# Layer 0's softmax with one exponential and sums on VectorE, and layer 1's head columns written by VectorE through a mask

## Chip, core and metric

The kernel runs on one core of a Trainium2 chip. The metric is the device time of one execution in microseconds (us). Five engines work side by side, each through its own queue of instructions in a fixed order: TensorE (PE, matrix products; its weight loads are listed as PEld), VectorE (DVE), ScalarE (ACT), GpSimd (POOL) and SyncE (SP, which here only issues transfers). An instruction waits, at the head of its queue, until the semaphores that it names have been raised by others.

## The reference, cut to what matters

Input x has 128 graphs of 64 nodes with 256 features, and all graphs share one adjacency matrix of 64x64. Four graph layers follow one another, each as `x = layernorm(x + layer(x))`. The change concerns the first two.

```python
# layer 0: attention over neighbours
Wh = h @ W
s1, s2 = Wh @ a1, Wh @ a2
e = s1[:, :, None] + s2[:, None, :]
e = where(e >= 0, e, 0.2 * e)
e = where(adj == 0, -inf, e)
h_prime = softmax(e, axis=-1) @ Wh

# layer 1: attention along 512 edges (src, dst), 4 heads of 64 features
Xq, Xv = H @ W_lin.T, H @ W_val.T                 # split into heads
e = einsum(leaky_relu(Xq[src] + Xq[dst], 0.2), a) + log(A0[src, dst] + 1e-8)
attn = softmax of e over the edges with the same src
Y = segment_sum(attn * Xv[dst], src) @ W_out.T
```

Layer 2 is a graph convolution with two batch norms, layer 3 two graph convolutions and four LSTMs with windows of 1 to 4 nodes; they take the last three quarters of the time and aren't touched.

## The kernel before

**Tiling.** Layers 0 and 1 run in one software pipeline over 16 blocks q. A block has 8 graphs: 512 tokens, as four chunks c of 128 tokens, so that a chunk holds two graphs (s = 0 in partitions 0 to 63, s = 1 in 64 to 127). Attention of layer 0 is computed for a chunk as one 128x128 matrix; `mask` is zero on the two 64x64 diagonal blocks where there is an edge, and -1e30 elsewhere.

**Layer 0 of a block** is in parts. `l0_a` (L238) turns x by a DVE transpose (L243). `l0_b` (L247) multiplies by W and copies the result out of PSUM by ACT (L255, L258). `l0_c` (L260) makes the scores e of [128, 4, 128] on DVE: sum with the mask (L267), leaky relu (L269), and the negated row maximum mx (L271). `l0_x` (L274) takes the exponential on ACT: one instruction for each of the four chunks, with mx as bias for each partition, and with the row sums collected by the same instruction (L278); the profile lists a READ_ACCUMULATOR after each. DVE then takes the reciprocal (L281). `l0_d` (L283) transposes the result on PE (L287) and copies it (L289, ACT). `l0_e` (L291) multiplies by Wh, scales and adds on DVE (L300) and normalises; `layernorm` (L88) does its statistics on DVE (L95, L96), a power on POOL (L86) and the scaling on POOL (L100).

**Layer 1 of a block.** `l1_t` (L310) transposes the tokens and copies them by ACT (L228). `l1_qv` (L314) makes queries and values of two chunks; it's called twice for a block. The product with wq (L324) has 260 columns: 256 queries and 4 head columns, a linear share of the score for each head. The queries go to `qs`, in two versions that hold one graph's rows as they are (a copy by ACT, L334) and for the other graph the remainder after rounding (a subtraction by DVE, L335). The head columns, times 0.2, go to `spad` (L336): one ACT instruction for each of the two graphs of a chunk, which writes the 4 columns of that graph's 64 rows; the other rows stay at the zero that they got at the start. The values (L327) are copied by ACT as `v` (L337). `l1_graph` (L356) gathers a graph's queries along the edges by a product with a one-hot matrix (L361, into one of two PSUM buffers z of two banks each) and applies relu on ACT (L363); `reduce_heads` sums over features (L352), and `l1_softmax`, `l1_sums`, `l1_weights` (L368 to L413) handle the softmax of two blocks together: a product with spad (L371), scans on DVE (L378 to L387), transposes (L395), reciprocal and weights on DVE (L401, L403), then a scatter into a table by POOL (L407) and a load back (L413). `v_a` (L422) multiplies values by weights (L432, copied by ACT as yT, L436), `v_b` (L438) multiplies by W_out (L446), adds (L448) and normalises, `v_c` (L454) multiplies by layer 2's adjacency (L467) and copies by ACT (L471).

**Order.** The loop over q (L701) has 8 steps, one for each graph of the block, and the table `between` (L703) says which parts of which other blocks come after each. S is the number of the pair of blocks whose layer 1 softmax is made in this step; it's there in even q from 2 on. In odd q, and in q=0, l0_x follows l0_c in the fifth group; in the other even q it stands in the sixth, after l1_qv, and `behind` (L692) orders it after the last ACT instruction recorded so far. `step` orders only PE: each part's first product comes after the part before it. A scheduler places the rest, engine by engine, as it estimates.

**Buffers.** Most products go into PSUM tiles called m, of one bank each, three in rotation (`bank`, L144): a product waits until every reader of the tile three before it is done.

Of the kernel before, what the change touches and what calls it, by code (L numbers as in the profile page):

```python
# [8 lines left out]
F32 = mybir.dt.float32  # L9
F32R = mybir.dt.float32r  # L10
I32 = mybir.dt.int32
AF = mybir.ActivationFunctionType
OP = mybir.AluOpType
AX = mybir.AxisListType
# [3 lines left out]
P = 128  # L18
NB = 128
N = 64  # L20
D = 256
KD = D // P
HEADS = 4
# [4 lines left out]
PQ = 4  # L28
QT = 512
GQ = 8  # L30
BPS = 2
# [6 lines left out]
SLOPE = 0.2  # L38
# [3 lines left out]
def kernel(ctx: ExitStack, tc: tile.TileContext, i, out):  # L42
    nc = tc.nc

    const = ctx.enter_context(tc.tile_pool(name="const", bufs=1))
    small = ctx.enter_context(tc.tile_pool(name="small", bufs=4))
# [83 lines left out]
    with ExitStack() as two:  # L130
# [5 lines left out]
        wa = two.enter_context(tc.tile_pool(name="wa", bufs=1))  # L136
# [7 lines left out]
        def bank(shape, name="m", bufs=3):  # L144
            return (psm if name == "m" else ps).tile([P] + shape, F32, name=name, bufs=bufs)
# [64 lines left out]
        count = wa.tile([P, EC], F32, name="count")  # L210
        place = wa.tile([P, EC], I32, name="place")
        spads = [wa.tile([P, P], F32, name=f"spad{n}") for n in range(2)]


        table = [dram.tile([PAIRS + E, SROWS], F32, name=f"table{n}") for n in range(2)]

        def own(q, shape, name):

            return work.tile(shape, F32, name=name, bufs=1) if q else su.tile(shape, F32, name)
# [16 lines left out]
        L0 = {}  # L236
# [37 lines left out]
        def l0_x(q):  # L274
            e, mx = L0[q]["e"], L0[q]["mx"]
            sm = small.tile([P, PQ], F32, name="sm")
            for c in range(PQ):
                nc.scalar.activation(e[:, c, :], e[:, c, :], AF.Exp, bias=mx[:, c:c + 1],  # L278
                                     accum_out=sm[:, c:c + 1])
            ri = L0[q]["ri"] = small.tile([P, PQ], F32, name="ri")  # L280
            nc.vector.reciprocal(ri, sm)  # L281

        def l0_d(q):  # L283
            e = L0[q]["e"]
            p_ = bank([PQ, P])
            for c in range(PQ):
                nc.tensor.transpose(p_[:, c, :], e[:, c, :], ident)  # L287
            eT = L0[q]["eT"] = own(q, [P, PQ, P], "eT")
            nc.scalar.activation(eT, p_, AF.Copy)  # L289
# [24 lines left out]
        def l1_qv(q, c2):  # L314
            xT, v = L1[q]["xT"], L1[q]["v"]

            sp = spads[q // BPS % 2].rearrange("p (s e x b d h) -> p s e x b d h", e=2, s=2, x=2, b=BPS, d=2)
            pv = None
            for c in (2 * c2, 2 * c2 + 1):
                pq = bank([D + HEADS])  # L320
                if pv is None:
                    pv = bank([2, D])
                for k in range(KD):
                    nc.tensor.matmul(pq, xT[:, k, c * P:(c + 1) * P], wq[:, k, :],  # L324
                                     start=k == 0, stop=k == KD - 1)
                for k in range(KD):
                    nc.tensor.matmul(pv[:, c % 2, :], xT[:, k, c * P:(c + 1) * P], wv[:, k, :],  # L327
                                     start=k == 0, stop=k == KD - 1)

                qs = work.tile([P, 2, D], F32R, name="qs", bufs=6)  # L330
                L1[q]["qs"].append(qs)
                for s in range(2):
                    r, ro = slice(s * N, (s + 1) * N), slice((1 - s) * N, (2 - s) * N)
                    nc.scalar.activation(qs[r, s, :], pq[r, :D], AF.Copy)  # L334
                    nc.vector.tensor_sub(qs[ro, s, :], pq[r, :D], qs[r, s, :].bitcast(F32))  # L335
                    nc.scalar.activation(sp[r, s, c % 2, 0, q % BPS, c // 2, :], pq[r, D:], AF.Copy, scale=SLOPE)  # L336
            nc.scalar.activation(v[:, 2 * c2:2 * c2 + 2, :], pv, AF.Copy)  # L337

        pes, pend = {}, []
# [26 lines left out]
        ld, sm = {}, {}  # L366
# [202 lines left out]
        setup_order()  # L569
        l0_c(0)  # L570
        l0_x(0)
        l0_a(1)
        setup_ends()
        l0_b(1)
        l0_d(0)
        setup_gather()
        setup_queries()
        l0_e(0)
        l0_c(1)
        l0_x(1)  # L580
        setup_signs()
        l0_d(1)
        l1_t(0)
        l1_qv(0, 0)
        l1_qv(0, 1)


# [91 lines left out]
        def step(do, n, *more):  # L679
            if not 0 <= n < NQ:  # L680
                return
            traced = nc.cur_bb.bb.instructions
            first = len(traced)
            if queue:
                with tc.issue_after(queue[-1]):
                    do(n, *more)
            else:
                do(n, *more)
            mine = [t for t in traced[first:] if t.engine == mybir.EngineType.PE]
            queue.extend(mine[-1:])  # L690

        def behind(do, q):  # L692
            if q < NQ:
                with tc.issue_after([t for t in nc.cur_bb.bb.instructions
                                     if t.engine == mybir.EngineType.Activation][-1]):
                    do(q)
# [4 lines left out]
        for q in range(NQ):  # L701
            S = q // BPS - 1 if q % BPS == 0 else -1
            between = [  # L703
                [(l0_e, q + 1), (l0_a, q + 2)],
                [(sums, q if q else -1), (l1_softmax, S)],
                [(l1_sums, S), (l0_b, q + 2)],
                [(v_b, q - LAG - 1)],
                [(l1_t, q + 1), (l1_weights, S), (l0_c, q + 2)] + [(l0_x, q + 2)] * (S < 0),
                [(sums, q), (l1_qv, q + 1, 0)] + [(lambda n: behind(l0_x, n), q + 2)] * (S >= 0),
                [(v_c, q - LAG - 1), (v_a, q - LAG)],  # L710
                [(l0_d, q + 2), (l1_qv, q + 1, 1)],
            ]
            for b in range(GQ):
                step(l1_graph, q, b)
                for do, n, *more in between[b]:
                    step(do, n, *more)
                if setup:
                    setup.pop(0)()
        sums(q)
        S = NQ // BPS - 1  # L720
# [256 lines left out]
        q = NQ - LAST - 1  # L977
# [16 lines left out]
        bias = wd.tile([P, SKIP, 8], F32, name="bias")  # L994
# [1010 lines left out]
```

## Time and profile before

| | |
|---|---|
| median of 3 runs | 2036.22 us (2034.6 to 2041.47) |
| the profiled execution's own time | 2039.12 us |
| its span, first to last instruction | 2037.3 us |
| mean granted clock of PE | 0.985 |

| stretch of the profiled execution (us) | what runs | PE busy | DVE busy | ACT busy | granted PE clock |
|---|---|---|---|---|---|
| 0 to 25 | loads, setup | 12.74 | 17.92 | 6.31 | 0.97 |
| 25 to 141 | setup, q = 0 to 2 | 98.67 | 68.45 | 70.94 | 0.92 |
| 141 to 475 | q = 3 to 13 | 318.73 | 197.08 | 225.10 | 0.99 |
| 475 to 525 | the last two q | 43.26 | 21.19 | 24.77 | 0.93 |
| 525 to 776 | layer 2 and the start of layer 3 | 240.97 | 144.18 | 112.65 | 0.97 |
| 776 to 2037.3 | layer 3 | 1225.69 | 799.18 | 548.23 | 1.00 |

The instructions that the change touches, over the whole execution or in the stretch from 125 to 475 us where that is said:

| line | engine, operation | shape | count | mean ns |
|---|---|---|---|---|
| L278, 125 to 475 | ACT exponential | 128x128 | 48 | 392 |
| L278, 125 to 475 | ACT read of the accumulator | 128x1 | 48 | 189 |
| L336, 125 to 475 | ACT head columns | 64x4 | 96 | 166 |
| L281, 125 to 475 | DVE reciprocal | 128x4 | 12 | 178 |
| L334, 125 to 475 | ACT copy of queries | 64x256 | 96 | 379 |
| L335 | DVE subtraction | 64x256 | 128 | 422 |
| L363 | ACT relu | 128x1024 | 128 | 1026 |

How to read it: the busy time of an engine in a stretch is the union of its instructions. In a line of the timeline come the start in us, the length in us, engine, line, operation, what it writes and reads, how many it merges, and in brackets the idle time of the engine before it with what ended it. In a list of waits come who waited for whom, the total in us, how often, and the longest. A row of the windows gives the stretch and its length, then for PE, PEld, DVE, ACT and POOL the busy time with the number of instructions, then PE's granted clock, the busy share of the transfer engines and GB/s.

### The profile page before, as it was taken

Reading aid. Unit: us, or ns where it says so; the run is one execution under the profiler, and the core shown is the slowest. Engines: PE = TensorE matmul, PEld = TensorE weight load, DVE = VectorE, ACT = ScalarE, POOL = GpSimd, SP = SyncE. Lnnn points to the kernel's source line nnn. Section 1 sums busy time; section 2 is a strip of 40 time slices with the busy share of each in tenths; the row PEclk is TensorE's granted clock in tenths of the full one; section 3 lists DMA queues with packets and bytes.
Section 4 is the critical chain, followed back from the end, with each engine's and each line's share of the span. In section 5 each row is a group of like instructions: output and inputs, shape, how many; then the busy total and the mean of one; then the engine's idle time right before and its main releaser. Section 6 shows DMA issues by size and latency. Waiting matters only on the chain.

```text
span 2037.3 us, 31496 instructions
## 1 busy us (share of the span) xinstructions
PE 1940.1 (95%) x11447; PEld 1337.8 (66%) x11447; DVE 1248.0 (61%) x2763; ACT 988.0 (48%) x1892; POOL 880.0 (43%) x1017
## 2 busy tenths in 40 slices
PE   5999999999999999899999999999999999999996
PEld 4667777766554445477678577667577668578685
DVE  7456565565456555765557865557775557664566
ACT  2766666666345633644343644333544333543333
POOL 1123333333445544564645543435543445444264
PEclk8999999999999998999999999999999999999999
DMA  5344443332302025433243243133143032132022
GB/s 129 85 67 65 83 68 55 66 45 39 51 22 60 38 93 185 148 139 107 86 162 92 66 155 136 39 132 88 58 152 121 24 111 66 47 119 78 0 62 73
DMA packets 236539, 173.84 MB, mean 85 GB/s; under 512 B 150624, under 2 KB 213600, under 8 KB 233056
## 3 DMA queue, kind: packets, MB, share of 16 engines
q1 hardware_dynamic: 234528, 169.86, 29.5%
q8 instruction: 90, 1.47, 0.3%
q0 software_dynamic: 1024, 1.05, 0.2%
q10 hardware_dynamic: 832, 0.92, 0.1%
q14 instruction: 65, 0.53, 0.1%
HBM read 110.18 MB, written 61.60 MB: 84 GB/s over the span
## 4 chain that ended last, share of the span: by engine, by line
PE 73%; DVE 14%; ACT 5%; DMA 3%; issue 3%; POOL 2%; SPq 1%; DVEq 0%; POOLq 0%; ACTq 0%
PE l L1728 27%; PE l L1684 8%; PE pz L845 4%; PE l L1463 4%; PE m L253 3%; PE pz L774 3%; PE m L324 3%; PE e L352 2%; PE m L446 2%; PE g L1362 2%; PE m L327 2%; PE z L361 2%; PE g L1350 2%; PE pz L1043 2%; DVE cell L1642 1%
## 5 line engine op out<-in xcount | busy, mean ns | idle before, releaser
L1728 PE MATMUL l<-hs,wh 128*128 128x256 f32 (+1 forms) x896 | 276.0, 399 | 3.7 <-DVE hs L1592 3.1
L1728 PE MATMUL l<-xs,wx 128*128 128x256 f32 (+1 forms) x896 | 276.2, 399 | 2.9 <-DVE gate L1747 2.7
L1743 ACT ACTIVATE kept<-l 128x256 f32<-128x256 f32 (+1 forms) x224 | 88.8, 403 | 333.2 <-PE l L1728 331.8
L86 POOL TENSOR_TENSOR ln_rs<-ln_rs,mhalf 128x2 f32<-128x2 f32 (+2 forms) x98 | 85.5, 873 | 367.4 <-DVE ln_rs L98 366.9
L1728 PE MATMUL l<-H,wx 128*128 128x256 f32 (+1 forms) x672 | 210.5, 402 | 4.3 <-DVE gate L1756 3.4
L1728 PE MATMUL l<-hid,wh 128*128 128x256 f32 (+1 forms) x672 | 208.7, 399 | 0.0
L1728 PEld LDWEIGHTS l<-hs,wh 128*128 128x128 f32 x896 | 169.1, 190 | 47.1 <-DVE hs L1592 5.7
L1728 PEld LDWEIGHTS l<-xs,wx 128*128 128x128 f32 x896 | 168.9, 190 | 46.1 <-issue 2.8
L1761 ACT ACTIVATE gate<-gate,bias 128x512 f32<-128x512 f32 (+1 forms) x280 | 170.6, 657 | 40.7 <-DVE gate L1752 34.8
L1684 PE MATMUL l<-H,wx 128*128 128x256 f32 (+5 forms) x672 | 185.2, 431 | 4.9 <-DVE H L116 2.7
L363 ACT ACTIVATE u<-z 128x1024 f32<-128x1024 f32 x128 | 130.3, 1026 | 68.8 <-PE z L361 67.7
L1684 PEld LDWEIGHTS l<-H,wx 128*128 128x128 f32 x672 | 118.8, 190 | 65.5 <-issue 34.2
L1728 PEld LDWEIGHTS l<-H,wx 128*128 128x128 f32 x672 | 125.7, 190 | 42.6 <-DVE gate L1756 7.4
L1728 PEld LDWEIGHTS l<-hid,wh 128*128 128x128 f32 x672 | 127.2, 190 | 32.0 <-issue 2.9
L1751 POOL TENSOR_TENSOR gate<-gate,kept 128x256 f32<-128x256 f32 (+1 forms) x84 | 65.1, 775 | 144.9 <-DVE kept L1749 136.2
L335 DVE TENSOR_TENSOR qs<-m,qs 64x256 fp32r<-64x256 f32 x128 | 54.0, 422 | 106.3 <-ACT qs L334 104.4
L361 PE MATMUL z<-gath_r,qs 128*128 128x512 f32 x256 | 100.4, 480 | 9.3 <-ACT u L363 8.9
L1756 DVE TENSOR_TENSOR gate<-l,gate 128x256 f32<-128x256 f32 (+1 forms) x112 | 50.0, 446 | 88.4 <-POOL gate L1751 64.3
L1596 POOL TENSOR_TENSOR hs<-hid 128x256 f32<-128x256 f32 (+1 forms) x28 | 26.0, 929 | 170.1 <-DVE hid L1628 87.0
L1650 ACT ACTIVATE gate<-cell 128x512 f32<-128x512 f32 (+1 forms) x88 | 58.6, 666 | 83.6 <-DVE cell L1642 61.5
L1638 POOL TENSOR_TENSOR cell<-gate,cell 128x512 f32<-128x512 f32 (+1 forms) x56 | 75.4, 1367 | 28.4 <-ACT gate L1761 28.4
L1745 DVE TENSOR_TENSOR gate<-l,kept 128x256 f32<-128x256 f32 (+1 forms) x112 | 49.1, 438 | 59.7 <-ACT gate L1761 32.6
(380 smaller groups left out, 4097.6 us busy)
## 6 DMA issues: line engine op xcount, KB each, us to landing
wx<-sums SPq DMA_DIRECT2D x9, 2048.0 KB
wh<-sums SPq DMA_DIRECT2D x9, 1792.0 KB
way<-st SPq DMA_DIRECT2D x54, 256.0 KB
st<-way SPq DMA_DIRECT2D x216, 64.0 KB
xin<-in_x SPq DMA_DIRECT2D x16, 512.0 KB
ld<-table SPq DMA_DIRECT2D x16, 512.0 KB
x_dram<-y SPq DMA_DIRECT2D x16, 512.0 KB
x2r<-x_dram SPq DMA_DIRECT2D x32, 256.0 KB
```

The source lines that it names most:

```text
L86: nc.gpsimd.tensor_tensor(dst, dst, mhalf[:, :n], OP.pow)
L253: nc.tensor.matmul(p_, xT[:, k, c * P:(c + 1) * P], w0[:, k, :], start=k == 0, stop=k == KD - 1)
L361: nc.tensor.matmul(z[:, k, :], L1[q]["qs"][c][:, s, k * P:(k + 1) * P], gath_r, start=True, stop=True)
L363: nc.scalar.activation(u, z, AF.Relu)
L845: nc.tensor.matmul(self.bank[at], lhs, rhs, start=first and n == 0, stop=n == len(self.terms) - 1, skip_group_check=True)
L1463: nc.tensor.matmul(self.bank[at], lhs, rhs, start=new, stop=True, skip_group_check=True)
L1638: nc.gpsimd.tensor_tensor(c, t, c, OP.mult)
L1684: nc.tensor.matmul(b, w.raw[0][:, k, at, m, :], x, start=k == 0, stop=k == KD - 1)
L1728: nc.tensor.matmul(self.banks[j], lhs, rhs, start=src == 0, stop=src == 1)
L1743: nc.scalar.activation(self.keep(j), b, AF.Copy)
L1751: e.tensor_tensor(t[0][:, 1], t[0][:, 1], k[5], OP.add)
L1761: given(lambda: nc.scalar.activation(dst, dst, f, bias=b))
```

## The change

Two edits, and one that follows from the first.

1. *Softmax of layer 0, blocks 2 to 15.* DVE adds the negated maximum to the whole e (512 elements a partition), ACT takes one exponential of the whole, and DVE sums the rows by a reduction. The sum and the reciprocal move from l0_x to l0_d, and the sum is ordered after the last DVE instruction recorded so far. Blocks 0 and 1 keep four exponentials with sums, but their reciprocal moves to l0_d too.
2. *Head columns.* A tile `slopes` of [128, 2, 4] holds 0.2 where the row belongs to graph s and 0 elsewhere; POOL writes it at the start. For each chunk one DVE product of the 4 columns (read twice from PSUM) with slopes writes the columns of both graphs, zeros included. The two ACT instructions are gone.
3. *Order.* l0_x now stands in the sixth group, after l1_qv and behind the last ACT instruction, in every q.

```diff
+        slopes = wa.tile([P, 2, HEADS], F32, name="slopes")
+        nc.gpsimd.memset(slopes, 0.0)
+        for s in range(2):
+            nc.gpsimd.memset(slopes[s * N:(s + 1) * N, s, :], SLOPE)
...
         def l0_x(q):
             e, mx = L0[q]["e"], L0[q]["mx"]
             sm = small.tile([P, PQ], F32, name="sm")
-            for c in range(PQ):
-                nc.scalar.activation(e[:, c, :], e[:, c, :], AF.Exp, bias=mx[:, c:c + 1],
-                                     accum_out=sm[:, c:c + 1])
+            if q < 2:
+                for c in range(PQ):
+                    nc.scalar.activation(e[:, c, :], e[:, c, :], AF.Exp, bias=mx[:, c:c + 1],
+                                         accum_out=sm[:, c:c + 1])
+            else:
+                nc.vector.tensor_add(e, e, mx[:, :, None].to_broadcast([P, PQ, P]))
+                nc.scalar.activation(e, e, AF.Exp)
+            L0[q]["sm"] = sm
+
+        def l0_d(q):
+            e, sm = L0[q]["e"], L0[q]["sm"]
             ri = L0[q]["ri"] = small.tile([P, PQ], F32, name="ri")
-            nc.vector.reciprocal(ri, sm)
-
-        def l0_d(q):
-            e = L0[q]["e"]
+            if q < 2:
+                nc.vector.reciprocal(ri, sm)
+            else:
+                with tc.issue_after([t for t in nc.cur_bb.bb.instructions if t.engine == mybir.EngineType.DVE][-1]):
+                    nc.vector.reduce_sum(sm, e, axis=AX.X)
+                nc.vector.reciprocal(ri, sm)
...
                     nc.scalar.activation(qs[r, s, :], pq[r, :D], AF.Copy)
                     nc.vector.tensor_sub(qs[ro, s, :], pq[r, :D], qs[r, s, :].bitcast(F32))
-                    nc.scalar.activation(sp[r, s, c % 2, 0, q % BPS, c // 2, :], pq[r, D:], AF.Copy, scale=SLOPE)
+                nc.vector.tensor_mul(sp[:, :, c % 2, 0, q % BPS, c // 2, :],
+                                     pq[:, None, D:].to_broadcast([P, 2, HEADS]), slopes)
...
-                [(l1_t, q + 1), (l1_weights, S), (l0_c, q + 2)] + [(l0_x, q + 2)] * (S < 0),
-                [(sums, q), (l1_qv, q + 1, 0)] + [(lambda n: behind(l0_x, n), q + 2)] * (S >= 0),
+                [(l1_t, q + 1), (l1_weights, S), (l0_c, q + 2)],
+                [(sums, q), (l1_qv, q + 1, 0)] + [(lambda n: behind(l0_x, n), q + 2)],
```

## The prediction, written before the changed kernel ran

> **What bounds the kernel now.** I read the page first (its shares of the span), then the windows by stage, then TensorE's waits in the stage that the change touches, and last the timeline of one even and one odd step of the loop over q.
>
> ```profile
> PE 1940.1 (95%) x11447; PEld 1337.8 (66%) x11447; DVE 1248.0 (61%) x2763; ACT 988.0 (48%) x1892; POOL 880.0 (43%) x1017
> ```
> ```profile
> 141.00:475.00 334.00, 318.73 (x2895) 234.97 (x2895) 197.08 (x517) 225.10 (x501) 121.18 (x137) 0.99 0.38 65
> ```
> ```profile
> PE z L361 <- ACT u L363: 8.6, 5, 1.8
> PE m L324 <- ACT yT L436: 4.0, 10, 0.6
> PE m L395 <- ACT tT L228: 1.5, 5, 0.3
> PE m L432 <- ACT v L337: 0.9, 1, 0.9
> ```
>
> TensorE (PE) sets the time: 95% of the span, and 318.7 of 334 us in the steady steps q=3 to q=13. So only PE's idle time there (15.3 us) and time lost to its clock can be won; ScalarE (ACT) and VectorE (DVE) each have a third of this stretch free. But all four waits of PE end on ACT. The largest comes five times, about 1.75 us each: PE waits for the relu L363, which frees one of the two z banks. In an even step (q=6):
>
> ```profile
> 246.33 0.81 PE L361 MATMUL z<-gath_r,qs 128*128 128x512 f32 x2
> 247.91 0.40 ACT L278 ACTIVATE e<-e,mx 128x128 f32<-128x128 f32 x1
> 249.89 1.02 ACT L363 ACTIVATE u<-z 128x1024 f32<-128x1024 f32 x1
> 250.81 1.02 ACT L471 ACTIVATE A<-z 128x1024 f32<-128x1024 f32 x1
> 250.96 0.75 PE L361 MATMUL z<-gath_r,qs 128*128 128x512 f32 x2 [1.79 <-ACT u L363]
> 251.71 1.09 ACT L436 ACTIVATE yT<-m 128x512 f32<-128x512 f32 x2
> 252.37 2.10 PE L324 MATMUL m<-wq,tT 128*128 128x260 f32 x4 [0.22 <-ACT yT L436]
> ```
>
> z was finished at 247.14, yet its relu began at 249.89: four exponentials and a head-column copy stood ahead of it in ACT's queue. Then the L324 group took 2.10 us; in the same place at 314.61 it takes 1.14. The windows row for 252.3 to 255.7 has PEclk at 0.50: the clock was halved after the stall. This happened in two of the five even steps (q=6 and q=10). In an odd step (q=7) the exponentials come early, the relu is just in time, and the remaining wait is for the first yT copy:
>
> ```profile
> 279.56 1.02 ACT L363 ACTIVATE u<-z 128x1024 f32<-128x1024 f32 x1
> 280.61 0.17 ACT L336 ACTIVATE spad<-m 64x4 f32<-64x4 f32 x1
> 280.80 1.03 ACT L471 ACTIVATE A<-z 128x1024 f32<-128x1024 f32 x1
> 282.37 1.15 PE L324 MATMUL m<-wq,tT 128*128 128x260 f32 x4 [0.56 <-ACT yT L436]
> ```
>
> [...] the trace has 392 (L278) and 629 (L381). [...] the trace has 692 (L373) and 868 (L380), and 686 for the reduction L271. [...] four L100 take 4.24 us under DVE's scans (230.64) and 2.17 without (264.25).
>
> **The change, part by part.** In the built program PE's order is the same but for one exchange of neighbouring pairs; ACT loses 170 instructions, DVE gains 92. In odd steps (and q=0, 1) the softmax also moves: its exponential now stands behind v of l1_qv's first half.
>
> *ACT, per step.* Four exponentials fill 275.79 to 277.43, 1.64 us; one of 0.63 replaces them: 1.0 saved. Eight head-column copies of 0.166 (L336) go: 1.3 saved. Off the path this is worth nothing; on it, only what follows.
>
> *DVE, per step.* An add of 512 (0.69 to 0.87 by the rows above; the trace has no such add with a broadcast operand, and I take 0.7), a reduction (0.69), four products of 8 elements from PSUM (0.17, as the 128x8 copy L539; 0.1 to 0.3). Together 2.1 us (1.8 to 2.4) on an engine that is busy 197 of 334. Cover: the add and first products lie in the first half of l1_qv, the reduction before the idle of 4.8 (even) and 4.5 us (odd) that DVE has ahead of the second half's first subtraction (L335 at 254.92 and 284.48). The products of the second half: the first falls into the 0.62 idle before 285.52, which itself shrinks because ACT's second copy no longer stands behind a head-column copy; the last delays L300 by at most 0.1. This matters, since from there DVE runs almost without a gap through the scans to L403 (242.93), which frees the bank for L324 at 242.94: no slack.
>
> *Waits.* The head-column copies waited for DVE's subtraction; now ACT's second and fourth copy wait for it themselves, with the third copy, v and the relu behind them. DVE's reduction waits for the exponential, with the reciprocal and the second half's subtractions behind it. [...] in odd steps it meets POOL's four L100 of y (274.41 to 276.58), needed by L467 at 278.47: up to 0.9 late, with 1.9 of slack. Costed at nothing, as are POOL's three new memsets (POOL idles 6.99 us before 9.76). No transfer is added; SP's order shifts slightly, but ACT's L471 waits only for loads that landed long before.
>
> *Even step, walked (q=6).* Third subtraction 246.88 becomes 247.05 (a product ahead of it), so the fourth copy runs 247.49 to 247.87. In the built order the relu now comes before the exponential: 247.89 to 248.91 instead of from 249.89. PE leaves L432 at 249.17 and no longer waits. The add ends by 248.3, exponential 248.8 to 249.43 (PE's transposes L287 follow at 249.5: a margin of 0.1), L471 249.35, first yT 250.25 to 250.85, so L324 at 250.91 instead of 252.37: 1.46 won. Next late is yT again, 0.4. Four such steps 5.8; q=4 waited less (1.50) and gives 1.2: **7.0**.
>
> *Odd step (q=7).* The add pushes the first subtraction from 275.92 to 276.07; the chain of copies and subtractions ends with v at 279.05 (was 278.76); exponential to 279.58, relu from 279.50 (was 279.56); no head-column copy before L471: 280.42, yT done at 281.92 instead of 282.33, L324 0.4 earlier. Five steps: **2.0**.
>
> *Clock.* The two halved stretches cost L324 0.96 and L327 0.70[...]: 1.5 each. Without stalls over 0.6 us I expect none: **3.0**.
>
> *First steps.* In q=0 and 1 the exponential now stands behind the fourth copy and v, so L287 is 0.2 later: -0.4. q=2: two waits for exponentials (0.84, 0.37) shrink by 0.4. q=3: v 0.35 earlier, and PE waits for it. Before the loop: the waits 2.39 (L324) and 0.48 (L327 for v) shrink by 0.7. Together **1.0**.
>
> Sum 13.0. The profiled execution took 2039.12 us (span 2037.3, 1.8 around it), so 2026.1. The median is 2.9 lower; perhaps it had one halved stretch fewer, then 2036.2 - 11.5 = 2024.7. I take 2025.5.
>
> **Rivals.**
> 1. *The wait only moves.* The margin of 0.1 before L287 is missed, or yT stays as late: then even steps give 0.5 (2.5), odd ones nothing, one halved stretch goes (1.5): -4, about 2033. For: PE already waits for yT in every step. Against: ACT sheds 2.3 us per step ahead of yT.
> 2. *More is won.* All of PE's idle in 141 to 475 (15.3), the clock (3.0) and about 2 before: -20, near 2018. Against: much of that idle is issue gaps of 0.3 us at L352 and L371.
> 3. *Slower: DVE becomes the bound.* The reduction blocks DVE's queue until the exponential ends; behind it stands the chain of subtraction, L243, L300, scans and L403 that ends at PE's L324 with no slack. It decides once exponential and reduction end more than 4.5 us later than walked. Then 2.1 us per step come onto the path, 14 times: +29, less the 13: 2052. For: even steps keep DVE busy 21.5 of 32. Against: the 4.5 to 4.8 us of idle.
> 4. *No effect.* Excluded as to what is built; as to time, PE's waits could be other than named: 2036.
>
> **Chances.** My forecast (2020 to 2031) 0.66, rival 2 0.08, rival 1 0.15 (a third of it beyond 0.3%), no effect 0.04, slower 0.07. A measurement of this kernel tells about 0.3% (6 us) from no change. Faster 0.66+0.08+0.05 = 0.79; same 0.10+0.04 = 0.14; slower 0.07. The range 2017 to 2033 holds the forecast, rival 2 and half of rival 1: 0.81.
>
> **What would show it.** Right: in the changed profile PE's wait for L363 in 141 to 475 is near 0 (8.6 now), the wait for yT 4 to 5 in ten pieces, no PEclk below 1.0 between 141 and 470, ACT about 32 us less busy over the loop, DVE about 29 more. Wrong: PE waits for L287's exponential or for L403's bank, or DVE's idle before the second half's first subtraction is gone.

## The result, and the profile after

The changed kernel took 2024.34 us (median of 6 runs, 2021.28 to 2026.47) beside 2038.41 us for the kernel before in the same comparison (6 runs, 2034.03 to 2041.47): ratio 0.9925, 95% interval 0.991 to 0.994. It is faster, by 14 us, close to the forecast 2025.5. Its profiled execution took 2025.54 us, with a span of 2023.8.

In the changed kernel lines have moved: L361 is now L376 (the gathering product), L363 L378 (relu), L324 L338 (queries), L334 and L335 L348 and L349, L436 L451 (yT), L471 L486 (A), L287 L301 (transposes of the exponential), L395 L410. L286 is DVE's new add, L287 the one exponential, L297 the reduction, L350 the head product.

The page's busy times, the windows row of the steady steps, and TensorE's waits there:

```profile
PE 1934.4 (96%) x11447; PEld 1336.6 (66%) x11447; DVE 1277.3 (63%) x2855; ACT 951.1 (47%) x1666; POOL 881.1 (44%) x1020
```
```profile
141.00:463.00 322.00, 315.74 (x2894) 232.94 (x2893) 219.17 (x582) 198.47 (x335) 123.30 (x137) 1.00 0.39 68
```
```profile
PE m L338 <- ACT yT L451: 4.2, 10, 0.6
PE m L410 <- ACT tT L232: 1.5, 5, 0.3
PE z L376 <- ACT u L378: 0.5, 2, 0.3
```

DVE gained 29.3 us, ACT lost 36.9, and neither number is the gain. What counts is the third fence: the wait for the relu fell from 8.6 us to 0.5, the wait for yT stayed (4.0, now 4.2), and the granted clock went from 0.99 to 1.00. PE is now idle for 6.3 us of this stretch (322.00 less 315.74), where it was 15.3 of 334.

The even step (q=6), where the relu used to stand behind four exponentials:

```profile
244.04 0.81 PE L376 MATMUL z<-gath_r,qs 128*128 128x512 f32 x2
245.63 1.02 ACT L378 ACTIVATE u<-z 128x1024 f32<-128x1024 f32 x1
246.55 0.62 ACT L287 ACTIVATE e<-e 128x512 f32<-128x512 f32 x1
246.81 0.73 PE L376 MATMUL z<-gath_r,qs 128*128 128x512 f32 x2
247.38 0.60 PE L301 MATMUL m<-ident,e 128*128 128x128 f32 x4
247.98 1.08 ACT L451 ACTIVATE yT<-m 128x512 f32<-128x512 f32 x2
248.63 1.15 PE L338 MATMUL m<-wq,tT 128*128 128x260 f32 x4 [0.65 <-ACT yT L451]
```

z was finished at 244.85 and its relu began 0.78 us later (2.75 before). The second L376 no longer waits, and the exponential, now behind the relu, ends at 247.17, 0.21 us ahead of the transposes L301. L338 took 1.15 us, at a granted clock of 1.00. What is late now is yT, as in the walk.

Step lengths tell more than the total. I measured each step from the first product of l0_b in one q to that in the next, in the profiled executions, us:

| kernel | to q=0 | q=0 | q=1 | q=2 | q=3 | even q, 4 to 12 | odd q, 5 to 11 | q=13 to 15 | rest |
|---|---|---|---|---|---|---|---|---|---|
| before | 61.5 | 29.02 | 23.84 | 29.70 | 25.06 | 31.38 (q=6: 32.84, q=10: 32.76) | 29.40 | 79.6 | 1511.3 |
| changed | 59.5 | 31.94 | 23.57 | 28.94 | 24.76 | 29.92 | 29.03 (q=7: 29.44, q=11: 29.19) | 78.0 | 1510.8 |
| difference | -2.0 | +2.9 | -0.3 | -0.8 | -0.3 | -1.46 (q=6: -2.91, q=10: -2.85) | -0.37 (q=7: +0.04, q=11: -0.21) | -1.5 | -0.5 |

The even steps together give -10.2, the odd ones -0.9. One number goes the wrong way: q=0 is 2.9 us *longer*. Its timeline:

```profile
75.88 0.60 ACT L352 ACTIVATE v<-m 128x512 f32<-128x512 f32 x1
76.48 1.28 ACT L287 ACT_TABLE_LOAD   x1
77.77 0.63 ACT L287 ACTIVATE e<-e 128x512 f32<-128x512 f32 x1
78.46 0.65 PE L301 MATMUL m<-ident,e 128*128 128x128 f32 x4 [2.09 <-ACT e L287]
```

This is the first exponential after the setup's logarithm (L660, which has a load of its own at 66.75). The table load in front of it (1.28 us) moved behind v together with the exponential. TensorE waits 2.09 us for the two. In the kernel before the same load lay in a gap of ACT ahead of the copies:

```profile
73.02 1.28 ACT L278 ACT_TABLE_LOAD   x1
74.32 0.40 ACT L278 ACTIVATE e<-e,mx 128x128 f32<-128x128 f32 x1
...
78.09 0.60 ACT L337 ACTIVATE v<-m 128x512 f32<-128x512 f32 x1
78.74 0.65 PE L287 MATMUL m<-ident,e 128*128 128x128 f32 x4 [0.34 <-ACT v L337]
```

There it cost TensorE nothing; the wait of 0.34 is for v. In the changed kernel a stretch of halved clock (granted 0.50, 3.4 us from 79.3) followed the stall.

### The profile page after: what moved, and what is told of

Its sections match the earlier page's. It is cut to its first block, busy times and chain, and to the rows that moved or that the text cites. A ratio compares the mean times of both kernels' runs of the same rounds, so it can differ in the third digit from the quotient of the medians.

```text
span 2023.8 us, 31384 instructions
## 1 busy us (share of the span) xinstructions
PE 1934.4 (96%) x11447; PEld 1336.6 (66%) x11447; DVE 1277.3 (63%) x2855; ACT 951.1 (47%) x1666; POOL 881.1 (44%) x1020
## 4 chain that ended last, share of the span: by engine, by line
PE 77%; DVE 14%; ACT 4%; issue 2%; POOL 1%; DMA 1%; SPq 0%; DVEq 0%; POOLq 0%; ACTq 0%
PE l L1743 29%; PE l L1699 8%; PE pz L860 4%; PE l L1478 4%; PE m L338 3%; PE pz L789 3%; PE m L257 3%; PE e L367 3%; PE z L376 2%; PE m L461 2%; PE m L341 2%; PE g L1377 2%; PE g L1365 2%; PE pz L1058 2%; DVE cell L1657 1%
## 5 line engine op out<-in xcount | busy, mean ns | idle before, releaser
L378 ACT ACTIVATE u<-z 128x1024 f32<-128x1024 f32 x128 | 130.0, 1025 | 71.9 <-PE z L376 71.3
L349 DVE TENSOR_TENSOR qs<-m,qs 64x256 fp32r<-64x256 f32 x128 | 54.0, 422 | 76.5 <-ACT qs L348 74.4
L376 PE MATMUL z<-gath_r,qs 128*128 128x512 f32 x256 | 99.5, 477 | 0.6 <-ACT u L378 0.5
```

What stands on the lines that cost most here:

```text
L376: nc.tensor.matmul(z[:, k, :], L1[q]["qs"][c][:, s, k * P:(k + 1) * P], gath_r, start=True, stop=True)
L378: nc.scalar.activation(u, z, AF.Relu)
```

## The experiments

My theory after the result: the even steps gain because ACT's relu of the seventh graph no longer stands behind four exponentials and a head-column copy, and it takes both parts of the change to get all of it; q=0 loses through the table load. Rivals: the new order alone did it (the softmax's form being beside the point); one part did all; DVE's new work is close to taking over. Eleven further runs were made, the last with the changed kernel itself. In the diffs "-" is the kernel named, before or changed.

### One part at a time, and the order alone

`e1_softmax_only` is the changed kernel with the head columns on ACT again, and without `slopes`:

```diff
-                nc.vector.tensor_mul(sp[:, :, c % 2, 0, q % BPS, c // 2, :],
-                                     pq[:, None, D:].to_broadcast([P, 2, HEADS]), slopes)
+                    nc.scalar.activation(sp[r, s, c % 2, 0, q % BPS, c // 2, :], pq[r, D:], AF.Copy, scale=SLOPE)
```

> Edits 1 and 3 alone: one exponential, sums on VectorE, softmax behind v; the head columns stay on ScalarE. Theory (TensorE's time is lost to what stands in ScalarE's queue ahead of the relu, of A and of yT): in even steps the relu comes 1.3 to 1.4 us earlier instead of 2.0, because one head-column copy and the exponential stay ahead of it; TensorE's wait for the relu falls from 1.75 to about 0.4, an even step gains about 1.2 and the clock stays whole (2.8); odd steps gain nothing or lose 0.1. The late table load still costs 2 to 3 us in q=0. Together -5 to -8 against the kernel before, so about half of the whole change. Rival (the head columns on VectorE are what matters, since each copy of queries stood behind one): no gain beyond 2 us. Rival (VectorE's extra work is the cost): with three quarters of that work left, this is slower than the whole change by less than 2 us.

`e2_heads_only` is the kernel before with the opposite edit: only the head columns on DVE, with slopes.

> Edit 2 alone: head columns on VectorE through the mask, the softmax as before with four exponentials. Theory: in even steps the four exponentials still stand ahead of the relu, which comes only 0.5 us earlier; TensorE's wait for it falls from 1.75 to about 1.2, an even step gains 0.5, an odd one 0.3 to 0.4 through yT, the steps before the loop 0.7 to 2, and the table load stays early. Whether the clock is still halved is left to chance. Together -5 to -8. If this and the softmax alone add to about the -14 of the whole change, the two edits act on the same queue one after the other. Rival (the softmax is all of it): within 2 us of the kernel before.

`e3_late_exp` is the kernel before with only an order changed: in even steps the four exponentials are issued behind the relu.

```diff
-                [(sums, q), (l1_qv, q + 1, 0)] + [(lambda n: behind(l0_x, n), q + 2)] * (S >= 0),
-                [(v_c, q - LAG - 1), (v_a, q - LAG)],
+                [(sums, q), (l1_qv, q + 1, 0)],
+                [(lambda n: behind(l0_x, n), q + 2)] * (S >= 0) + [(v_c, q - LAG - 1), (v_a, q - LAG)],
```

> The kernel before with one thing changed: in even steps with a layer 1 softmax the four exponentials are ordered behind the relu of the seventh graph, nothing is made cheaper. Rival (the gain is only the order of relu and exponentials): -10 or more, as the 1.75 us waits go and the clock stays whole. Theory (ScalarE must have less to do ahead of yT): the relu's wait goes, but TensorE then waits for the exponentials at the transposes and for yT as late as before, so that L324 begins at the same time; 0 to -3, the latter if shorter waits spare the halved clock.

| kernel | median us | ratio to before, 95% interval | even q | odd q | q=0 |
|---|---|---|---|---|---|
| e1_softmax_only | 2033.0 (19 runs) | 0.9973 (0.9963 to 0.9982) | 30.53 | 29.54 | 32.22 |
| e2_heads_only | 2025.63 (6 runs) | 0.9944 (0.9926 to 0.9963) | 31.06 | 28.65 | 28.22 |
| e3_late_exp | 2039.35 (14 runs) | 1.0005 (0.9993 to 1.0017) | 31.39 (two at 32.9) | 29.40 | 29.01 |

The kernel before took 2038.17 on the same chip. The first lines of TensorE's waits from 141 to 463 us, for e1 (L371 and L373 are the gathering product and its relu, L334 and L446 the queries and yT), e2 (L366, L368; L328, L441) and e3 (the numbers of before):

```profile
PE z L371 <- ACT u L373: 5.4, 10, 0.6
PE m L334 <- ACT yT L446: 3.9, 10, 0.6
```
```profile
PE z L366 <- ACT u L368: 7.0, 5, 1.5
...
PE m L328 <- ACT yT L441: 1.4, 6, 0.2
```
```profile
PE m L324 <- ACT yT L436: 8.3, 9, 1.2
```

e1 (-5.2 us) came at the edge of what my theory had (-5 to -8; an even step gains 0.86 where 1.2 was expected), and e3 (+1.2, within its interval) as it had it. e3 disposes of the order alone: the wait for the relu vanished from its list, the wait for yT doubled in its place (from 4.0 in ten pieces to 8.3 in nine), and the time is the same. ACT's queue between z and yT must become *shorter*, not only different. e1 shortens it by 1.0 us and gets 0.86 an even step; with the head-column copies still on ACT the relu is awaited ten times, 0.6 at most. e2 alone gets only 0.33 an even step, since the relu still stands behind four exponentials (7.0 us in five waits). Both together get 1.46, more than 0.86 + 0.33: each part by itself leaves the relu late. One thing more differs: in e1 the exponential stands ahead of the relu in ACT's queue (247.03 and 247.68 us), in the changed kernel behind it (246.55 after 245.63). No run separates this exchange from the rest, so the surplus of 0.27 may be due to it.

The median of e2 was a miss: -12.5 us where -5 to -8 was expected. Its steps show where from: odd steps gain 0.75, twice what the whole change has; q=1 gains 1.0 and q=2 2.5; two stretches of halved clock (q=6, q=10) are absent, 2.8, though the stall that they followed is only 0.3 us shorter. So part of this median depends on where the halved stretches fell. The gain of the odd steps doesn't: the whole change loses in odd steps half of what its second part wins. That asked for a further test (below).

### The table load

`e4_early_table` is the changed kernel with one exponential of a tile of [128, 4] added in l0_c of block 2, whose result nobody reads, so that the table is loaded early:

```diff
             L0[q]["mx"] = mx
+            if q == 2:
+                nc.scalar.activation(small.tile([P, PQ], F32, name="ri"), mx, AF.Exp)
```

> The changed kernel with one tiny exponential of the row maxima (4 elements, result unused) in l0_c of block 2, so that the table of the exponential is loaded in ScalarE's gap before the first copy of queries, as it was before the change. Theory (in q=0 the change lost 2.9 us because the 1.28 us load moved into the queue between v and the exponential, made TensorE wait 2.09 us and halved its clock): q=0 is 2 to 3 us shorter, the time is 2 to 3 us below the changed kernel, about 0.991 of the kernel before. Rival (q=0 lost its time to VectorE's new work or to the softmax's new place alone): less than 0.7 us better.

Measured 2021.16 us (6 runs; 2038.17 for the kernel before on this chip), ratio 0.992 (0.9903 to 0.9937); q=0 took 28.84 us, 3.1 less than in the changed kernel. In its q=0 the timeline of ACT has the load ahead of the copies, and TensorE waits a third as long:

```profile
69.32 1.28 ACT L278 ACT_TABLE_LOAD   x1
...
74.22 0.60 ACT L354 ACTIVATE v<-m 128x512 f32<-128x512 f32 x1
74.71 0.62 ACT L289 ACTIVATE e<-e 128x512 f32<-128x512 f32 x1
```
```profile
PE m L303 <- ACT e L289: 0.7, 1, 0.7
```

The step shows the cause of the longer q=0; the total alone would not, for the ratio's interval overlaps the changed kernel's (0.991 to 0.994). How much of the 3.1 is the load itself: a second profile of the changed kernel (e11 below) has the same wait of 2.09 without a halved clock in q=0, and a q=0 of 30.25. So in these profiles 1.4 us is the load and 1.7 the clock that it may or may not drag along.

### Where the odd steps lose: three mixtures

`e5_mixed` keeps the head columns on DVE everywhere, but the new softmax only in even steps; odd ones and q=0 have the four exponentials in the fifth group as before. `e6_mixed_swap` is e5 with v_a ahead of v_c, so that ACT copies yT before A. `e7_new_fifth` is the changed kernel with its order alone undone. Their diffs against the changed kernel (e5: both; e7: the second only) and of e6 against e5 (the condition on q stands twice, in l0_x and in l0_d; one is shown):

```diff
-            if q < 2:
+            if q < 4 or q % 2:
...
-                [(l1_t, q + 1), (l1_weights, S), (l0_c, q + 2)],
-                [(sums, q), (l1_qv, q + 1, 0)] + [(lambda n: behind(l0_x, n), q + 2)],
+                [(l1_t, q + 1), (l1_weights, S), (l0_c, q + 2)] + [(l0_x, q + 2)] * (S < 0),
+                [(sums, q), (l1_qv, q + 1, 0)] + [(lambda n: behind(l0_x, n), q + 2)] * (S >= 0),
```
```diff
-                [(v_c, q - LAG - 1), (v_a, q - LAG)],
+                [(v_a, q - LAG), (v_c, q - LAG - 1)],
```

> The change with the softmax's new form only in even steps (the softmaxes of blocks 4, 6, 8, 10, 12 and 14); all other blocks keep the four exponentials with their sums, issued in the fifth group of products as before the change; the head columns on VectorE everywhere. Theory (the gain is a sum over steps: new form pays in even steps only, head columns pay in odd ones): even steps 29.9 us as in the changed kernel, odd ones 28.65 as in the kernel with the head columns alone (29.03 in the changed kernel), q = 0 about 28.2 since the table of the exponential is loaded ahead of v again; together 5 to 7 us below the changed kernel: 2016 to 2019 us. Rival (the two parts share one wait, so the odd steps were short in the heads-only kernel only because of its long even ones): odd steps stay near 29.0 and the time at 2020 to 2022.

> As the mixed kernel, with the products of yT issued ahead of those of A in the seventh group, so that on ScalarE the two copies of yT (0.60 us each) stand ahead of the copy of A (1.02). Theory (what is late after the change is the copies of yT: 0.4 us in each even step): the wait of L338's products for yT is gone and even steps are 0.3 to 0.5 us shorter, 2 to 3 us in all against the mixed kernel. Rival (the next thing stands just behind: the copy of A holds a buffer of z, so that the product of the eighth graph or the transposes wait in its place): within 1 us of the mixed kernel, or up to 5 slower, with a wait for A in the records.

> The changed kernel with one thing undone: in odd steps and q = 0 the softmax (in its new form) is issued in the fifth group of products again, not behind ScalarE's last instruction of the sixth. Theory of place (odd steps lost 0.38 us each against the heads-only kernel because the exponential was moved behind the relu and v): odd steps 28.6 to 28.7 us, q = 0 about 28.3 to 28.8 with the table loaded early, and 5 to 6 us below the changed kernel: 2018 to 2020. Theory of form (the one exponential waits for VectorE's add, 0.7 us later than the four would start, whatever its place): odd steps 29.0 or more, and only q = 0 better: 2021 to 2023, or more if the relu of the sixth graph then waits behind the exponential (up to 0.7 us in each odd step).

| kernel | median us (4 runs each) | ratio to before, 95% interval | even q | odd q | q=0 |
|---|---|---|---|---|---|
| e5_mixed | 2017.76 | 0.9887 (0.987 to 0.9903) | 29.92 | 28.65 | 28.21 |
| e6_mixed_swap | 2017.61 | 0.9886 (0.9869 to 0.9902) | 29.91 | 28.65 | 29.77 (a halved stretch in it) |
| e7_new_fifth | 2017.51 | 0.9882 (0.9866 to 0.9899) | 29.92 | 28.66 | 29.86 |

All three lie 6 to 7 us below the changed kernel's 2024.3, and the intervals of the ratios don't meet (0.9903 at most here, 0.991 at least there). e5 came as its theory had it. e7's even and odd steps came as its theory of place had them; its q=0 did not (29.86, where 28.3 to 28.8 was expected). e7 settles the cause: with the new form in the old place the odd steps are at 28.66, as with the old form (e5) and as in e2. So the place costs the odd steps 0.37, not the form. In q=1 it costs more: 23.57 in the changed kernel, 22.85 in e5 and e7. The same stretch of an odd step (q=9) in the changed kernel, then in e7:

```profile
333.15 0.62 ACT L287 ACTIVATE e<-e 128x512 f32<-128x512 f32 x1
333.68 1.02 ACT L378 ACTIVATE u<-z 128x1024 f32<-128x1024 f32 x1
334.58 1.03 ACT L486 ACTIVATE A<-z 128x1024 f32<-128x1024 f32 x1
335.49 1.09 ACT L451 ACTIVATE yT<-m 128x512 f32<-128x512 f32 x2
336.14 1.14 PE L338 MATMUL m<-wq,tT 128*128 128x260 f32 x4 [0.23 <-ACT yT L451]
```
```profile
323.29 0.63 ACT L287 ACTIVATE e<-e 128x512 f32<-128x512 f32 x1 [0.17 <-DVE e L286]
...
326.36 1.02 ACT L378 ACTIVATE u<-z 128x1024 f32<-128x1024 f32 x1
327.29 1.02 ACT L486 ACTIVATE A<-z 128x1024 f32<-128x1024 f32 x1
328.19 1.09 ACT L451 ACTIVATE yT<-m 128x512 f32<-128x512 f32 x2
328.85 1.15 PE L338 MATMUL m<-wq,tT 128*128 128x260 f32 x4
```

In e7 the exponential runs in the middle of the copies of queries, where ACT has gaps, and nothing stands between them and the relu; L338 comes without a wait. In the changed kernel it comes directly ahead of the relu, A and yT, and TensorE waits 0.23 for yT.

e6 shows that the remaining wait in even steps can't be won by exchanging the two copies: the steps are unchanged, and the place of the wait for yT is taken by the next copy in ACT's queue (L303 is the copy of the transposed exponential):

```profile
PE m L338 <- ACT eT L303: 2.3, 5, 0.5
```

The rival for e6 held, though with eT and not A as the one that is late.

### How much cover has VectorE

The forecast costed DVE's 2.1 us a step at nothing, with its idle time ahead of the second half's first subtraction (4.8 and 4.5 us) as cover. Two kernels add to the one reduction of a block the same reduction again, 3 and 8 times (the sums are the same):

```diff
                     nc.vector.reduce_sum(sm, e, axis=AX.X)
+                    for _ in range(3):
+                        nc.vector.reduce_sum(sm, e, axis=AX.X)
```

> The changed kernel with VectorE's reduction of 512 elements (0.69 us) issued four times in place of once in each of 14 blocks, the same sums each time: 2.07 us more on VectorE in each step, 29 us in all, at the place where VectorE's queue waits for the exponential. VectorE is idle 4.5 to 4.8 us in a step. Theory (VectorE's added work is covered by its idle time): no change, 2022 to 2027 us; at most 0.3 us in a step. Rival (the reduction blocks the queue: the subtractions of the second half of the queries stand behind it, and PE's banks behind those): each further 0.69 us shows up in the step, up to 29 us more, 2040 to 2053.

> The same with nine reductions in place of one: 5.5 us more on VectorE in each of 14 steps, 77 us in all, about 1 us more than its idle time in a step. Theory (covered until the idle time is used up): 0.7 to 1.5 us more in a step and 10 to 20 in all, 2035 to 2045 us, with PE waiting for VectorE. Rival (blocked queue): the products wait for the subtractions and banks by 3 to 5.5 us in a step, 45 to 77 us in all, 2070 to 2100 us.

e8: 2026.14 us (4 runs), ratio 0.9958 (0.9941 to 0.9974), even 29.93, odd 29.03: in its profile 2.07 us more of DVE in a step lengthen no step from q=5 on by more than 0.03, and q=1 and q=4 by 0.12. (The profiled execution is the fastest of the four, and the ratio's interval lies just above the changed kernel's, 0.991 to 0.994, so a small loss in the total isn't excluded.) e9: 2068.23 (4 runs), ratio 1.0159 (1.0142 to 1.0176), *slower* than the kernel before; odd steps 30.67 (+1.64), even ones 33.94, and 32.30 in the one without a halved stretch (+2.38). Its first line of waits from 141 to 463 us shows who is late (L313 is l0_e's product with Wh, L352 the head product):

```profile
PE m L313 <- DVE spad L352: 15.4, 10, 2.1
```

The head product is the last reader of a bank m; it stands in DVE's queue behind the subtractions, these behind the reductions, and TensorE wants the bank. That is the third rival of the forecast, made to happen, though TensorE waits at L313 and not at the queries' product that the rival named. With 5.52 us added, and if each us beyond the cover costs one, the cover left over was 3.1 us in even and 3.9 in odd steps. The changed kernel's trace has the same: DVE's idle time ahead of the second half's first subtraction (first an even step, q=6, then an odd one, q=5), and 0.45 more ahead of the second, together 3.07 and 3.98.

```profile
250.73 0.42 DVE L349 TENSOR_TENSOR qs<-m,qs 64x256 fp32r<-64x256 f32 x1 [2.62 <-ACT qs L348]
```
```profile
219.93 0.42 DVE L349 TENSOR_TENSOR qs<-m,qs 64x256 fp32r<-64x256 f32 x1 [3.53 <-ACT qs L348]
```

The stretch from 141 to 463 us of the changed kernel has 9.3 us of DVE idle a step (102.8 over 11 steps); a third or a little more of that is cover. Both my theory (2035 to 2045) and the rival (2070 to 2100) missed e9: the wait is the rival's, its size lies between, and the clock added some 1.6 us to four of the five even steps.

### The best version, beside the changed kernel on one chip

`e10_best` is e7 with the old form for block 2 too (`q < 3`), since in e7's q=0 the new form delays v (the table load and the one exponential stand between the copies of queries there, from 71.22 to 73.15 us). `e11_after_again` is the changed kernel itself.

> The changed kernel with its order undone in odd steps and q = 0 (the softmax in the fifth group there) and the softmax's old form for block 2 as well as 0 and 1. Theory (the change's order costs 0.38 us in odd steps and 3 in q = 0; the new form for block 2 costs q = 0 another 1.6, because ScalarE's one exponential waits for VectorE's add): odd steps 28.65, even ones 29.92, q = 0 28.2, and 6 to 8 us below the changed kernel on the same chip, 1 to 2 below the kernel whose one edit is the order undone. Rival (the time of q = 0 to 2 and of the last steps is set by where the stretches of the halved clock fall): within 1 us of that kernel, still 5 to 7 below the changed one.

> The changed kernel itself once more, for a comparison on the same chip with the version that undoes its order. Theory: 2024 us, a ratio of 0.992 to 0.994 against the kernel before, 6 to 8 us above that version. Rival (the difference between them came from different chips): less than 3 us above it.

e10: 2018.27 us (5 runs), ratio 0.9893 (0.9875 to 0.9911); e11: 2024.45 us (6 runs), 0.9921 (0.9903 to 0.994). On one chip the version with the order undone is 6.2 us below the changed kernel, as expected. The two profiles differ by 7.9 us in span, and the steps that were edited account for 4.8 of it: q=0 gives 2.0, q=1 0.7, q=5, 9 and 11 together 1.1, q=7 1.1, and q=3 takes back 0.2. Most of the rest lies where the two kernels are alike (1.3 before the loop, 1.4 in the layers behind it). Against e7 it won nothing that can be measured: its q=0 is 1.6 us shorter (28.22), as expected, but q=2 is 1.7 us longer (28.93, with a halved stretch at 127.9 us that e7 didn't have). So the rival held on this point.

## Why the prediction was right, point by point

*What bounds the kernel, and the even steps (-7.0): right.* Walked 1.46 a step, measured 1.46 in q=8 and q=12, and 1.48 in q=4, where I had said 1.2: 7.3 without the clock. The order of what is late next (yT) was right, and the margin of 0.1 before the transposes was 0.21. e1, e2 and e3 show that the reason was right too: not the order, but the work ahead of yT in ACT's queue. The signs that the forecast named came: over the loop ACT is 35.0 us less busy (32 forecast) and DVE 28.9 more (29), and the next halved stretch starts at 471.9 us, just behind the 470 that it named.

*Clock (-3.0): right in size, in part by luck.* No stretch of halved clock from 141 to 463 us; q=6 and q=10 gained 1.45 and 1.39 beyond the others. Of the thirteen profiles, the nine whose longest wait of TensorE in this stretch is 0.7 us or less have no halved stretch in it. Of the four with longer waits, three have two or more (before 1.8 us, e3 1.2, e9 2.1), and e2, with stalls of up to 1.5, has none. So a stall makes one possible, not certain. The forecast's limit of 0.6 us was an estimate. In the traces of before and of the changed kernel all halved stretches start at multiples of 3.41 us from one another (in the changed kernel at 24.7, 38.4, 52.0, 79.3 and 133.9 us, for example). What decides whether one starts was not shown: in the last 3.41 us ahead of the halved stretch of q=10 (from 371.77) TensorE was busy for 1.64 us, and in the same stretch of the grid in q=8 (from 310.33) and q=12 (from 433.21) for 1.65 each, with no halved clock behind it. The number of such stretches also differs between runs of one kernel: the 32 runs of the kernel before on one chip have mean clocks from 0.981 to 0.988. At a mean clock of 0.987 on the chip of e11, the changed kernel took 2023.9 and 2024.4 us and the kernel before 2035.8 to 2036.1, so about 12 us of the gain are there at an equal clock.

*Odd steps (-2.0): direction right, size too large.* Walked 0.4, measured 0.37 in q=5 and q=9, 0.30 in q=3 and 0.21 in q=11; in q=7 nothing, in part because TensorE waited 0.28 for the relu as well: 1.2 together. What I had not seen is that 0.37 is a difference: the head columns give 0.75 (e2, e5, e7) and the new place of the exponential takes half of it back. The walk had the exponential's end just before the relu and took that as free ("relu from 279.50, was 279.56"); the right comparison was with the change without its third edit.

*First steps (-1.0): this step of the forecast failed.* For q=0 it said +0.2, because the exponential stands behind the fourth copy and v. It was +2.9 in this execution and +1.2 in another. I counted what the moved exponentials cost and overlooked the ACT_TABLE_LOAD in front of the first, which the profile of before shows in one line. In both traces the load stands directly in front of the first exponential (at 73.02 before, at 76.48 in the changed kernel), and in e4 in front of the small one added there (the load at 69.32, that exponential at 70.62): in each of these kernels the 1.28 us went where the first exponential went. (In the changed kernel v ends at 76.48, the load runs from there to 77.76 and the exponential starts at 77.77; of the 3.1 us that e4 won, 1.4 are left without the clock.) Elsewhere the first steps gained more than forecast: 0.3 in q=1, 0.8 in q=2, and 2.0 before the loop, where 0.7 was forecast. Little of that last number belongs to the change: e3, whose code there is that of before, was 1.8 us shorter in its profile too, and like the changed kernel it has 13.7 us of halved clock there, the kernel before 17.1.

*DVE costs nothing: right, with 1 us less cover than named in even steps.* The add took 0.69 to 0.78 us (I took 0.7; two operations of the same size in the trace of before, the add L373 and the subtraction L380, have medians of 0.69 and 0.87), the reduction 0.69, the head product 0.17. In the odd steps the add ran beside POOL's four L100 of y, as walked: together they took 2.59 us (in q=7 from 269.73) where it was 2.17, so 0.42 of the 0.9 that I had estimated, and no wait of TensorE for them is in the list. e8 shows that 2.07 more is free in the steady steps; e9 that beyond 3 to 4 us it isn't. With the reduction that the change itself puts there (0.69), that is a cover of 3.8 us in even and 4.6 in odd steps, where 4.8 and 4.5 were named.

*The sum.* Forecast -13.0 against the profiled execution, measured -13.5 in span. Part of the agreement is a cancellation: the missed 2.7 of q=0 and the 0.8 too much in the odd steps stand against 1.3 more before the loop and 1.5 in q=13 to 15, for which I had forecast nothing. Both kernels have two halved stretches in q=13 to 15, so that this 1.5 may well belong to the change; with one to four such stretches the same steps took 76.4 to 81.9 us in the kernels of this study without added sums, and I haven't taken them apart. *Rivals:* the first fell, since an even step gained 1.46 and not 0.5; the time of the second (near 2018) was reached by e7, but by another way than it named; the third is real, but needs more than 3 us more of DVE work in a step.

## What to carry to other kernels

When an instruction is moved or merged, move everything that hangs on it: here the table load before the first exponential took 1.28 us, the instruction itself 0.63. Judge each part of a change by the step that it lies in: here the late place of the exponential, which the even steps had already, cost the odd ones 0.37 us, and the version that undoes it there, with the old form for block 2, was another 6 us faster in the median (in the profiles the edited steps show some 5 of them). And the cover of added work is the idle time in front of the instruction that someone waits for (3 to 4 us were left over here), not the idle time of the engine in the step (9.3).

## What the runs showed of the hardware

- Four exponentials of 128 elements with sums took 1.64 us (0.39 each, and 0.19 for each read of the accumulator, which overlap in part); one of 512 took 0.62 to 0.63. DVE's add of 512 with a broadcast operand took 0.69 to 0.78, its product of 8 elements from PSUM with a repeated operand 0.17.
- In one execution of the kernel before, the clock was halved after two of the five stalls of the even steps (1.5 to 1.8 us each) and not after the other three; in this trace and in that of the changed kernel all halved stretches (granted 0.50) start on one grid of 3.41 us. A step in which one fell was 1.4 to 1.7 us longer. Between kernels whose first steps differ by 1 or 2 us these stretches fall elsewhere, and can hide such a difference, as between e7 and e10.
- q=7 was 0.3 to 1.0 us longer than the other odd steps in six profiles (29.44 and 30.06 in two of the changed kernel, 29.05 in e2), and q=11 0.2 in two. The cause stays open.
